# Attention with its probabilities turned on VectorE, values as 32x32 products in the scores' banks, and w_q and w_o streamed

## The chip, the cores and the metric

The kernel runs on one core of one Trainium2 chip. The metric is the device time of one launch in microseconds. Three runs of the kernel before took 1241.42 us in the median (1240.85 to 1242.42).

The engines are TensorE (in the profile PE for products and PEld for the loading of weights into the array), VectorE (DVE), ScalarE (ACT), GpSimd (POOL) and SyncE (SP), which issues all of this kernel's DMAs in one queue. Each engine works through its own instructions in the order in which the program gives them, and waits for others by semaphores. SBUF is the working memory with 128 partitions; PSUM, into which TensorE writes, has eight banks of 512 f32 columns in each partition.

## The reference, cut

All is f32. x is 4 sequences of 512 tokens with 1024 features; 32 query heads and 8 key/value heads of 32 features; 8 experts with low-rank weights of rank 16, of which each token uses 2.

```python
x = x + layernorm(attn(layernorm(x)))
x = x + layernorm(ffn(layernorm(x)))

def attn(x):
    q, k, v = split(x @ w_qkv.T + b_qkv)          # 1024, 256, 256 columns
    q, k = rope(q), rope(k)
    k, v = repeat(k, 4), repeat(v, 4)             # four query heads share one key head
    s = q @ k.T / sqrt(32), causal mask
    return (softmax(s) @ v) @ w_o.T + b_o

def ffn(x):
    top-2 gate over x @ gate_w.T; w = its softmax
    return x @ base_w.T + base_b + 2 * sum_e w[e] * (x @ A[e].T) @ B[e].T
```

## The kernel before

**Tiles.** A token tile is 128 tokens, 16 in all, four to a sequence. For each, TensorE computes keys and values (acc_kv), queries (acc_q, two halves of 512 columns), attention, the output projection (acc_o, two halves), the gate and low-rank inputs (acc_gl) and the base product (acc_f, two halves). Such a half is eight products of 128x128 weights-in-array by 512 columns, summed in one PSUM bank (`project`, L520 to L545). Activations are turned by TensorE against an identity before a projection (pt_xn, pt_h, pt_q, pt_k).

**Attention.** Heads are laid out so that a k tile (kt, two of them) holds four key heads, one on each quarter of the partitions, and a q tile holds one query head for each of these. `scores` (L1050) computes for a group of q tiles (four, two or one, as many as fill 512 columns with (i+1)*128 keys, where i is the token tile's place in its sequence): products of 32 rows, four side by side, into the tile sc of pool ps_sc. That is one tile of four banks, so one group of scores is alive at a time. VectorE masks the diagonal (L1119) and takes the negative maximum (L1129); ScalarE takes the exponentials into pr with their sum (L1079); VectorE inverts the sum (L1088); GpSimd multiplies (L1093). `turn` (L1138) turns pr on TensorE in 128x128 pieces (L1143) into a bank, and ScalarE or VectorE copies it to SBUF as prT (`copy`, L323 to L329). `values` (L1156) multiplies prT with v, 128 rows by 32 columns of the array, four heads side by side (L1166), and the result is copied to aT.

**Weights.** w_qkv and w_o are loaded whole once (`all_loads`, L1190). w_base is streamed: `Stream` (L393) loads pieces of 128x512 f32 (256 KB) into a ring of RING = 8, each as soon as a place is free; 256 pieces in all.

**Order.** The order of every engine is written out while the program is built. `Order` (L89) keeps a clock with an estimate for each instruction. TensorE's steps (`Step`, L79) stand in lanes: scores, turns of activations, values (with the turns of the probabilities), and dense products. `_choice` (L198) takes the first lane that is ready and `tensor` (L232) issues it; a score step and a ready value step go out as a pair (PAIRED). Instructions of the other engines are taken by urgency, then by age (`_next`, L138). Buffers are counted by `Slots` (L50): a chain takes a slot before it issues and gives it back when its last reader is done. BANKS = 4 PSUM banks outside the scores' serve all other products; SOFT = 10 tiles serve pr and prT.

Of the kernel before, what the change touches and what calls it, by code (L numbers as in the profile page):

```python
# [11 lines left out]
F32 = mybir.dt.float32  # L12
# [4 lines left out]
P = 128  # L17
# [15 lines left out]
PAIRED = 0.55  # L33
# [45 lines left out]
class Step:  # L79


    def __init__(self, us, issue, needs=(), bank=False, soon=()):
        self.us, self.issue, self.needs = us, issue, list(needs) + list(soon)
        self.tiled = False
        self.bank, self.soon = bank, soon
        self.done = Task()


class Order:  # L89
    ENGINES = ("dve", "act", "pool", "sp")  # L90

    def __init__(self, banks):
        self.now = self.at = 0.0
        self.free = dict.fromkeys(self.ENGINES, 0.0)
        self.waiting = {e: [] for e in self.ENGINES}
        self.seq = 0
        self.banks = banks
# [75 lines left out]
    def _ready(self, step):  # L173
        at = 0.0
        for t in step.needs:
            if t.at is None:
                return None
            at = max(at, t.at)
        if step.bank:
            if not self.banks.free:  # L180
                return None
            at = max(at, self.banks.free[0])
        return at

    def _take(self, step):
        if step.bank:
            heapq.heappop(self.banks.free)
        step.issue()

    def _is_ready(self, step):  # L190
        at = self._ready(step)
        return at is not None and at <= self.now

    def _comes(self, step):

        return all(t.at is not None for t in step.needs if t not in step.soon)

    def _choice(self, scores, values, lanes):  # L198

        later, ready, last = [], [], []  # L200
        score = scores[0] if scores else None


        value = values[0] if values and values[0].tiled else None
        waiting = []
        if score is not None and value is not None:
            if self._comes(score):
                waiting.append(values)
            if self._comes(value) and not self._is_ready(value):
                waiting.append(scores)  # L210
        for lane in lanes:
            at = self._ready(lane[0])
            if at is None:
                continue
            later.append(at)
            if at <= self.now:
                if any(lane is w for w in waiting):
                    last.append(lane)
                elif at + SAFE <= self.now:
                    return lane, None  # L220
                else:
                    ready.append(lane)
        if ready or last:
            return (ready + last)[0], None
# [7 lines left out]
    def tensor(self, scores, urgent, values, dense):  # L232


        while True:
            self.run(self.now)
            dense = [lane for lane in dense if lane]
            lanes = [lane for lane in [scores, *urgent, values] if lane]
            lanes += sorted(dense, key=lambda lane: lane[0].bank)
            if not lanes:  # L240
                break
            lane, at = self._choice(scores, values, lanes)
# [3 lines left out]
            steps = [lane.pop(0)]  # L246
            us = steps[0].us + TILING * steps[0].tiled
            if lane is scores and values and values[0].tiled and self._is_ready(values[0]):
                steps.append(values.pop(0))
                us = steps[0].us + steps[1].us + PAIRED  # L250
            for step in steps:
                self._take(step)
            self.now += us
            for step in steps:
                step.done.finish(self.now + FILL)
# [4 lines left out]
def kernel(  # L260
# [27 lines left out]
    BANKS, SOFT, RING = 4, 10, 8  # L288
# [7 lines left out]
    soft = ctx.enter_context(tc.tile_pool(name="soft", bufs=SOFT))  # L296
    weights = ctx.enter_context(tc.tile_pool(name="weights", bufs=RING))
# [6 lines left out]
    banks = Slots(BANKS)  # L304
    soft_slots, act_slots = Slots(SOFT), Slots(4)
    qT_slots, kT_slots, raw_slots, turn_slots = Slots(3), Slots(3), Slots(2), Slots(1)
    xa_slots, y_slots, w_slots = Slots(1), Slots(2), Slots(2)
    order = Order(banks)
# [42 lines left out]
    wqkv_sb = const.tile([P, ND, QKV], F32, name="wqkv_sb")  # L351
    rope_sb = const.tile([P, NQ, 2, HD], F32, name="rope_sb")
    bqkv_sb = const.tile([P, QKV], F32, name="bqkv_sb")
    wo_sb = const.tile([P, ND, D], F32, name="wo_sb")
# [13 lines left out]
    def chunks(name, w_sb, w, at, n):  # L368
        return [
            load(  # L370
                (name, at, c),
                P * n * 4 / 1024,
                w_sb[:, c, at : at + n],
                w[c * P : (c + 1) * P, at : at + n],
            )
            for c in range(ND)
        ]

# [10 lines left out]

    def part(w_sb, at, n):  # L390
        return lambda c: w_sb[:, c, at : at + n]

    class Stream:  # L393
# [10 lines left out]
        def __init__(self, w, n):  # L404
            self.w, self.n, self.slots, self.pieces = w, n, Slots(n), []

        def ask(self, c, cols):
            piece = self.Piece(self, self.w[c * P : (c + 1) * P, cols])
            self.pieces.append(piece)
            return piece  # L410

        def run(self, after):
# [4 lines left out]
            yield after  # L417
            for k, piece in enumerate(self.pieces):
                yield self.slots.take()

                def issue():
                    piece.sb = weights.tile([P, 512], F32, tag="piece", name=f"piece_{k}")
                    nc.sync.dma_start(out=piece.sb, in_=piece.in_)
# [4 lines left out]
    base_stream = Stream(w_base, RING)  # L428


    class Norm:
# [16 lines left out]
        def scale(self):  # L448
# [13 lines left out]

            yield dve(0.2, self.urgent, aggr)
            yield dve(0.15, self.urgent, eps)
            yield pool(0.6, 0, root)

        def apply(self, dst, src, h):
            cols = slice(h * 512, (h + 1) * 512)
            yield dve(
                0.7,  # L470
                self.urgent,
                lambda: nc.vector.tensor_scalar(  # L472
                    dst()[:, cols],
                    src()[:, cols],
                    self.mv[:, 0:1],
                    self.rstd,
                    ALU.subtract,
                    ALU.mult,
                ),
            )  # L480
# [13 lines left out]
    def transposes(dst, src, halves, name, slot):  # L494
# [3 lines left out]
        for h in range(NH):  # L498
# [17 lines left out]
            steps.append(Step(0.44, issue, [halves[h], slot], bank=True))  # L516
# [3 lines left out]
    def project(lhsT, w, n, name, needs, take, more=None):  # L520
# [20 lines left out]
        for c in range(ND + (more is not None)):  # L541
            us = 0.858 if n == 512 else 0.24
            steps.append(Step(us, partial(issue, c), needs[c], bank=(c == 0)))
# [3 lines left out]
    def rotated(acc, b_at, n, i, name, urgent, hold):  # L547
# [3 lines left out]
        yield raw_slots.take()  # L551
# [50 lines left out]
    class Tokens:  # L602
        def __init__(self, t):
# [3 lines left out]
            self.aT, self.has_aT = None, [Task() for _ in range(ND)]  # L607
# [46 lines left out]
    def load_y(tok):  # L654

        yield y_slots.take()
        yield has_wqkv
# [9 lines left out]
    def qkv(job, has_k, has_q):  # L667
# [6 lines left out]
        def normed():  # L674
# [4 lines left out]
            for h in range(NH):  # L679
                yield from norm.apply(lambda: job.xn, lambda: job.xn, h)  # L680
# [26 lines left out]
        def take_kv(acc, done):  # L707
# [3 lines left out]
            has_v = seq.has_v[i]  # L711

            def v_issue():
                seq.v[i] = kvpool.tile([P, KVD], F32, tag="v", bufs=6, name=f"v_{t}")
                nc.vector.tensor_add(
                    seq.v[i], acc[:, KVD : 2 * KVD], bqkv_sb[:, D + KVD : D + 2 * KVD]
# [3 lines left out]
            has_v.finish(order.at)  # L720
            yield from rotated(acc, D, KVD, i, f"k_{t}", 2, raw_k)
            k_ready.finish(order.at)

# [20 lines left out]
        step_k = Step(0.23, turn_k, [k_ready] + seq.kT_taken, bank=True)  # L744
        raw_q, q_ready = [[] for _ in range(NH)], [Task() for _ in range(NH)]

        def take_q(h, acc, done):
# [4 lines left out]
            yield qT_slots.take()  # L752
# [19 lines left out]
        steps_q = [Step(0.44, partial(turn_q, h), [q_ready[h]], bank=True) for h in range(NH)]  # L772

        def needs(at, n):
            return [
                [ready[c // 4]] + ([loaded["qkv", at, c]] if not t else []) for c in range(ND)
            ]

# [5 lines left out]
        products, turned = [], []  # L784
        if has_k:
            products += project(
                xnT, part(wqkv_sb, D, 2 * KVD), 2 * KVD, f"kv_{t}", needs(D, 2 * KVD), take_kv
            )
            turned.append(step_k)
        if has_q:  # L790
            for h in range(NH):
                products += project(
                    xnT,
                    part(wqkv_sb, h * 512, 512),
                    512,
                    f"q_{t}_{h}",
                    needs(h * 512, 512),
                    partial(take_q, h),
# [5 lines left out]
    def attention_out(tok):  # L804
# [50 lines left out]
        first = [loaded["o", 0, c] for c in range(ND)]  # L855
        steps = []
        for h in range(NH):
            needs = [
                ([tok.has_aT[ND - 2], slot] if not c else [tok.has_aT[c]])
                + ([first[c]] if not t else [])  # L860
                for c in range(ND)
            ]
            steps += project(
                lambda: tok.aT,
                part(wo_sb, h * 512, 512),
                512,
                f"o_{t}_{h}",
                needs,
                partial(take, h),
# [45 lines left out]
    def ffn(tok):  # L915
# [52 lines left out]
        step_low = Step(0.11, turn_low, [low_in], bank=True)  # L968
# [14 lines left out]
        def out_half(h):  # L983
            yield from norm.apply(lambda: tok.w, lambda: tok.w, h)
# [12 lines left out]
        def rest():  # L997
# [14 lines left out]
            part(wgl_sb, 0, GL),  # L1012
            GL,
            f"gl_{t}",
            [[r, loaded["gl"]] if not t else [r] for r in (ready[c // 4] for c in range(ND))],
            take_gl,
        )
        f = []
        for n in range(NH):
            cols = slice(n * 512, (n + 1) * 512)  # L1020
            chunks_n = [base_stream.ask(c, cols) for c in range(ND)]
            wants = [[ready[c // 4], chunks_n[c].here] for c in range(ND)]
# [332 lines left out]
```

## Time and profile before

| | us |
|---|---|
| median of three runs | 1241.42 |
| the profiled execution | 1241.56 |
| its span, first to last instruction | 1239.8 |
| PE busy | 1210.3 |
| DVE busy | 809.4 |
| POOL busy | 455.5 |
| ACT busy | 434.6 |
| HBM read | 97.94 MB |
| mean granted TensorE clock | 0.995 |

The span is what the profile covers. Busy times of an engine are the union of its instructions. The chain of waits is followed back from the last instruction to what released each one, so its shares tell which engine's work set the end. In a group's row, "128*32 128x128" means 128 rows by 32 columns of the array, 128 partitions by 128 columns streamed; "x2560" counts records, and an f32 product has two of them, one for each pass; the turns have one.

### The profile page before, as it was taken

The numbers are of one execution on the slowest core, as the hardware profiler recorded it, in microseconds if no ns is written. First come the engines' busy times: TensorE is split into PE (matmuls) and PEld (weight loads), VectorE is DVE, ScalarE is ACT, GpSimd is POOL, SyncE is SP. The second block draws the span as 40 slices with busy tenths as digits, with TensorE's granted clock in tenths as the row PEclk, the third lists the DMA queues.
The fourth block names the chain that finished last, engine by engine and source line by source line (L and its number), as shares of the span: only waits on it lengthen the run. The fifth ranks groups of instructions, "written<-read, shape, count | busy, mean of one in ns | idle before, by whom it ended". The sixth has DMA issues, their size and how long they took to land.

```text
span 1239.8 us, 20306 instructions
## 1 busy us (share of the span) xinstructions
PE 1210.3 (98%) x7416; PEld 658.6 (53%) x7416; DVE 809.4 (65%) x1673; ACT 434.6 (35%) x1360; POOL 455.5 (37%) x696
## 2 busy tenths in 40 slices
PE   7999999889999999999999999999999999999997
PEld 3555555445555555555555555555555555555543
DVE  3676766567657575866747667766666666777653
ACT  0343433334334333334444334323325333344400
POOL 1344434234154442424345334333234342434411
PEclk9999999999999999999999999999999999999999
DMA  9600050221410414113141140040411304105334
GB/s 359 248 18 17 2 165 23 69 77 43 136 52 8 145 36 133 55 36 119 35 128 61 52 137 17 15 148 26 136 52 52 120 1 136 35 23 163 131 110 152
DMA packets 54369, 107.63 MB, mean 87 GB/s; under 512 B 6400, under 2 KB 7424, under 8 KB 54272
## 3 DMA queue, kind: packets, MB, share of 16 engines
q1 hardware_dynamic: 54272, 106.36, 26.3%
q8 instruction: 59, 0.97, 0.3%
q14 instruction: 38, 0.31, 0.1%
HBM read 97.94 MB, written 8.39 MB: 86 GB/s over the span
## 4 chain that ended last, share of the span: by engine, by line
PE 95%; DVE 2%; ACT 1%; POOL 1%; issue 0%; DMA 0%; POOLq 0%; SPq 0%; ACTq 0%; DVEq 0%
PE acc_f L531 20%; PE acc_q L531 17%; PE acc_o L531 17%; PE pt_p L1143 12%; PE acc_kv L531 9%; PE sc L1058 7%; PE av L1166 6%; PE acc_gl L531 2%; PE pt_xn L505 1%; PE pt_h L505 1%; PE pt_q L758 1%; ACT pr L1079 1%; DVE nmax L1129 0%; PE pt_k L727 0%; DVE prT L328 0%
## 5 line engine op out<-in xcount | busy, mean ns | idle before, releaser
L1093 POOL TENSOR_SCALAR pr<-pr,rtot 128x256 f32<-128x256 f32 (+3 forms) x512 | 288.6, 577 | 519.5 <-DVE rtot L1088 426.6
L1079 ACT ACTIVATE pr<-sc,nmax 128x256 f32<-128x256 f32 (+3 forms) x512 | 263.5, 535 | 161.7 <-DVE nmax L1129 140.2
L531 PE MATMUL acc_f<-piece,T_h 128*128 128x512 f32 x512 | 236.5, 597 | 2.3 <-ACT prT L327 1.4
L531 PE MATMUL acc_o<-wo_sb,aT 128*128 128x512 f32 x512 | 233.3, 593 | 0.0
L531 PE MATMUL acc_q<-wqkv_sb,T_xn 128*128 128x512 f32 x480 | 220.7, 595 | 0.0
L1129 DVE TENSOR_REDUCE nmax<-sc 128x4 f32<-128x1536 f32 (+5 forms) x98 | 185.9, 1897 | 10.1 <-ACT pr L1079 8.4
L327 ACT COPY prT<-pt_p 128x512 f32<-128x512 f32 (+1 forms) x192 | 103.4, 551 | 245.8 <-PE pt_p L1143 240.1
L1143 PE MATMUL pt_p<-ident,pr 128*128 128x128 f32 x1280 | 177.0, 276 | 9.2 <-ACT prT L327 2.9
L1143 PEld LDWEIGHTS pt_p<-ident,pr 128*128 128x128 f32 x1280 | 146.6, 141 | 74.2 <-issue 63.3
L328 DVE COPY prT<-pt_p 128x512 f32<-128x512 f32 (+1 forms) x160 | 101.8, 637 | 62.4 <-PE pt_p L1143 59.6
L531 PEld LDWEIGHTS acc_o<-wo_sb,aT 128*128 128x128 f32 x512 | 92.4, 190 | 92.6 <-issue 91.3
L531 PEld LDWEIGHTS acc_f<-piece,T_h 128*128 128x128 f32 x512 | 91.7, 191 | 90.8 <-issue 84.8
L531 PEld LDWEIGHTS acc_q<-wqkv_sb,T_xn 128*128 128x128 f32 x480 | 86.3, 191 | 82.6 <-issue 80.9
L531 PE MATMUL acc_kv<-wqkv_sb,T_xn 128*128 128x512 f32 x256 | 119.1, 599 | 0.0
L1079 ACT ACTIVATION_READ_ACCUMULATOR pr<-sc,nmax 128x1 f32 x512 | 108.9, 213 | 0.0
L1058 PE MATMUL sc<-kT,qT 32*128 32x384 f32 (+3 forms) x1024 | 94.8, 468 | 0.0
L1088 DVE RECIPROCAL rtot<-total 128x1 f32<-128x1 f32 (+2 forms) x352 | 53.3, 158 | 61.4 <-ACT pr L1079 59.1
L487 POOL TENSOR_TENSOR y<-y,w 128x512 f32<-128x512 f32 x60 | 78.5, 1321 | 35.4 <-DVE w L472 35.4
L1166 PEld LDWEIGHTS av<-prT,v 128*32 128x32 f32 x2560 | 64.6, 109 | 50.0 <-issue 43.3
L1166 PE MATMUL av<-prT,v 128*32 128x128 f32 x2560 | 88.2, 276 | 0.0
L1119 DVE TENSOR_TENSOR sc<-sc,cmask 128x512 f32<-128x512 f32 (+3 forms) x98 | 83.7, 854 | 4.9 <-PE sc L1058 4.0
L461 POOL TENSOR_TENSOR rstd<-veps,neg_half 128x1 f32<-128x1 f32 x64 | 36.3, 567 | 125.1 <-DVE veps L457 111.3
(83 smaller groups left out, 898.9 us busy)
## 6 DMA issues: line engine op xcount, KB each, us to landing
piece<-in_w_base_dram SPq DMA_DIRECT2D x256, 256.0 KB, 3.4
xa<-in_x_dram SPq DMA_DIRECT2D x32, 256.0 KB, 3.0
y<-in_x_dram SPq DMA_DIRECT2D x16, 512.0 KB, 3.6
out_dram<-y SPq DMA_DIRECT2D x32, 256.0 KB, 2.0
wqkv_sb<-in_w_qkv_dram SPq DMA_DIRECT2D x8, 512.0 KB, 8.9
wo_sb<-in_w_o_dram SPq DMA_DIRECT2D x8, 512.0 KB, 7.3
wqkv_sb<-in_w_qkv_dram SPq DMA_DIRECT2D x8, 256.0 KB, 5.1
bqkv_sb<-in_b_qkv_dram SPq DMA_DIRECT2D x1, 768.0 KB, 7.7
```

The source lines that it names most:

```text
L327: act=(0.15 + n * 0.00085, lambda: nc.scalar.copy(out(), in_())),
L328: dve=(0.15 + n * 0.00105, lambda: nc.vector.tensor_copy(out(), in_())),
L487: engine.tensor_tensor(out=y()[:, cols], in0=y()[:, cols], in1=z()[:, cols], op=ALU.add)
L531: nc.tensor.matmul(acc[0][:, :n], lhsT=lhsT()[:, c, :] if c < ND else more[0](), rhs=w(c) if c < ND else more[1], start=(c == 0), stop=last,)
L1058: nc.tensor.matmul(sc[:, r, c * n : (c + 1) * n], lhsT=tok.qT[g.kt][rows, (g.at + c) % GROUP, :], rhs=seq.kT[g.kt][rows, :n], start=True, ...
L1079: lambda: nc.scalar.activation(pr[:, c * n : (c + 1) * n], sc4[:, r, c, :], AF.Exp, bias=nmax[:, r, c : c + 1], accum_out=total[:, r, c : ...
L1088: yield dve(0.17, 1, lambda: nc.vector.reciprocal(rtot[:, r, : g.n], total[:, r, : g.n]))
L1093: lambda: nc.gpsimd.tensor_scalar(pr[:, c * n : (c + 1) * n], pr[:, c * n : (c + 1) * n], rtot[:, r, c : c + 1], 1.0, ALU.mult, ALU.mult,),
L1119: lambda: nc.vector.tensor_tensor(out=diag, in0=diag, in1=cmask.unsqueeze(1).unsqueeze(1).to_broadcast([P, q, g.n, P]), op=ALU.add,),
L1129: lambda: nc.vector.tensor_reduce(nmax[:, some, : g.n], sc4[:, some], AX.X, ALU.max, negate=True),
L1143: nc.tensor.transpose(pt[:, j, :], g.pr[r][:, j * P : (j + 1) * P], ident)
L1166: nc.tensor.matmul(av[r * HD : (r + 1) * HD, c, :], lhsT=g.seq.v[j][:, head * HD : (head + 1) * HD], rhs=g.prT[r][:, c * (i + 1) + j, :], ...
```

## The change

- **Probabilities.** `turn` and its copies go. After the multiplication on GpSimd, VectorE's transpose instruction turns each 32x32 block of pr into z, the blocks staying where they are (`quadrant`). Four tiles z (one for each of the four heads of a k tile) hold all four q tiles of a k tile: pool zpool, one set of four.
- **Values.** One step for each k tile of a token tile (`Set`) in place of one for each group. For each block of 32 keys (4(i+1) of them) there are 16 products of 32x32 of the array by 128 columns: a quarter of the array's rows for each block of 32 queries, a quarter of its columns for each head. They write into a tile of ps_sc, so the scores' banks hold either a group of scores or a set of values. v has to lie on every quarter of the partitions: `spread` copies it with 16 DMAs of 32x256 for each token tile.
- **Weights.** w_q and w_o are streamed as w_base is, each through a ring of its own, RING = 6 for all three; only the key and value columns stay resident.
- **Norm.** It adds a negated mean where it subtracted the mean, and the pass over xa, and over w behind the ffn (but for the last tile), may run on GpSimd as well as on VectorE.
- **Order.** Score and value steps are no longer paired or held back for each other; values come first, then scores, then the rest. A projection starts only when there are slots for its results (`room_for`). Two inverses of the sums are taken at once (`totals`). The last two groups are no longer exchanged. SOFT goes from 10 to 8.

```diff
-    BANKS, SOFT, RING = 4, 10, 8
+    BANKS, SOFT, RING = 4, 8, 6
+    zpool = ctx.enter_context(tc.tile_pool(name="zpool", bufs=QUADS))
...
+    sc_slots, z_slots = Slots(1), Slots(QUADS)
...
-    wqkv_sb = const.tile([P, ND, QKV], F32, name="wqkv_sb")
+    wkv_sb = const.tile([P, ND, 2 * KVD], F32, name="wkv_sb")
-    wo_sb = const.tile([P, ND, D], F32, name="wo_sb")
...
+    streams = {"q": Stream("q", w_qkv), "o": Stream("o", w_o), "f": Stream("f", w_base)}
+
+    def streamed(name, at, steps):
+        pieces = streams[name].ask(at)
+        made = steps(lambda c: pieces[c].sb, [piece.here for piece in pieces])
+        for piece, step in zip(pieces, made):
+            start(piece.used(step.done))
+        return made
...
+            def minus():
+                self.nmean = small.tile([P, 1], F32, tag="nmean", bufs=4, name=f"nmean_{name}")
+                nc.vector.tensor_scalar_mul(self.nmean, self.mv[:, 0:1], -1.0)
...
+            on = {"dve": (0.7, partial(issue, nc.vector))}
+            if either:
+                on["pool"] = (0.8, partial(issue, nc.gpsimd))
+            yield Op(self.urgent, **on)
...
+        def spread(v):
+            seq.v[i] = kvpool.tile([P, QUADS, KVD], F32, tag="vq", bufs=6, name=f"vq_{t}")
+            for b in range(QUADS):
+                for r in range(QUADS):
+                    yield sp(
+                        0.09,
+                        lambda: nc.sync.dma_start(
+                            out=seq.v[i][r * HD : (r + 1) * HD, b, :],
+                            in_=v[b * HD : (b + 1) * HD, :],
+                        ),
+                    )
+            yield LANDS
+            seq.has_v[i].finish(order.at)
...
-            g.normed[r].finish(order.at)
+            yield g.set.has_room
+            at = (g.at % GROUP) * n
+            yield dve(
+                0.1 + g.n * n * 0.00105,
+                1,
+                lambda: nc.vector.transpose(g.set.z[r][:, at : at + g.n * n], pr[:, : g.n * n]),
+            )
+            soft_slots.give(order.at)
...
-    def turn(g, r):
...
-        for j in range(m):
-            nc.tensor.transpose(pt[:, j, :], g.pr[r][:, j * P : (j + 1) * P], ident)
...
-    def values(g):
+    def values(s):
...
-        av = ps.tile([P, GROUP, P], F32, tag="ps", name=f"av_{g.name}")
...
+        av = ps_sc.tile([P, QUADS, 512], F32, tag="sc", name=f"av_{s.name}")
+        nb = QUADS * (i + 1)
+        for b in range(nb):
+            for r in range(QUADS):
+                head = s.kt * GROUP + r
+                z = s.z[r][:, : GROUP * (i + 1) * P]
+                z = z.rearrange("p (c b q) -> p c b q", c=GROUP, b=nb)
+                for quad in range(QUADS):
+                    rows = slice(quad * HD, (quad + 1) * HD)
                     nc.tensor.matmul(
+                        av[r * HD : (r + 1) * HD, quad, :P],
+                        lhsT=s.seq.v[b // QUADS][rows, b % QUADS, head * HD : (head + 1) * HD],
+                        rhs=z[rows, :, b, :],
+                        start=(b == 0),
+                        stop=(b == nb - 1),
                     )
...
+            needs = [tok.has_q[one.kt]] + keys
+            older = k - 1 if m else k - 2
+            if older >= 0:
+                needs.append(sets[older].valued.done)
+            us = 0.218 * g.n * (tok.i + 1) + TILING
+            g.scored = Step(us, partial(scores, g), needs, bank=sc_slots)
+            score_lane.append(g.scored)
+        needs = [one.full, tok.aT_taken] + [tok.seq.has_v[i] for i in range(tok.i + 1)]
+        us = 0.92 * (tok.i + 1) + TILING
+        one.valued = Step(us, partial(values, one), needs, bank=sc_slots)
...
-    order.tensor(score_lane, turn_lanes, value_lane, dense_lanes)
+    order.tensor([value_lane, score_lane, *turn_lanes], dense_lanes)
```

## The prediction

> **What bounds the kernel now.** I read the page's busy shares and its chain of waits first, then the groups by shape, then one stretch of the timeline, the DMA issues, and a table of two tiny windows.
>
> ```profile
> PE 1210.3 (98%) x7416; PEld 658.6 (53%) x7416; DVE 809.4 (65%) x1673; ACT 434.6 (35%) x1360; POOL 455.5 (37%) x696
> PE 95%; DVE 2%; ACT 1%; POOL 1%; issue 0%; DMA 0%; POOLq 0%; SPq 0%; ACTq 0%; DVEq 0%
> PE acc_f L531 20%; PE acc_q L531 17%; PE acc_o L531 17%; PE pt_p L1143 12%; PE acc_kv L531 9%; PE sc L1058 7%; PE av L1166 6%; PE acc_gl L531 2%; PE pt_xn L505 1%; PE pt_h L505 1%; PE pt_q L758 1%; ACT pr L1079 1%; DVE nmax L1129 0%; PE pt_k L727 0%; DVE prT L328 0%
> ```
>
> TensorE (PE) is the chain: 95% of 1239.8 us. The turning of the probabilities (pt_p) is 12% of it, about 148 us, and all of that leaves TensorE with this change. The question is what comes next.
>
> ```profile
> 289.00 1.14 PE L1058 MATMUL sc<-kT,qT 32*128 32x512 f32 x8
> ...
> 290.20 0.70 DVE L1119 TENSOR_TENSOR sc<-sc,cmask 128x512 f32<-128x512 f32 x1
> 290.94 2.29 DVE L1129 TENSOR_REDUCE nmax<-sc 128x4 f32<-128x2048 f32 x1
> ...
> 293.56 1.07 ACT L327 COPY prT<-pt_p 128x512 f32<-128x512 f32 x2 [0.71 <-PE pt_p L1143]
> ...
> 294.52 0.70 ACT L1079 ACTIVATE pr<-sc,nmax 128x512 f32<-128x512 f32 x1
> ...
> 295.73 0.59 ACT L327 COPY prT<-pt_p 128x512 f32<-128x512 f32 x1 [0.41 <-PE pt_p L1143]
> ...
> 298.12 0.22 ACT L1079 ACTIVATION_READ_ACCUMULATOR pr<-sc,nmax 128x1 f32 x1
> ...
> 299.86 1.14 PE L1058 MATMUL sc<-kT,qT 32*128 32x512 f32 x8
> ```
>
> This is one group of scores (one of four q tiles of a k tile, 512 keys) in the timeline of all engines. It holds the scores' four banks from 289.00 to 298.34, 9.34 us, and the next group can't start before. The reader is to see the parts: product, wait for VectorE, mask, maximum, wait for ScalarE (busy with prT copies), four exponentials with another prT copy between. Taking all 88 groups from the timeline the same way, the mean hold is 16.3 us (128 keys, 8 groups), 12.7 (256, 16), 8.9 (384, 32) and 10.2 (512, 32): 945 us of banks in use. Before, that has slack against TensorE.
>
> ```profile
> L1143 PE MATMUL pt_p<-ident,pr 128*128 128x128 f32 x1280 | 177.0, 276 | 9.2 <-ACT prT L327 2.9 <-DVE rtot L1088 2.7 <-POOL pr L1093 2.6
> L1166 PE MATMUL av<-prT,v 128*32 128x128 f32 x2560 | 88.2, 276 | 0.0
> L328 DVE COPY prT<-pt_p 128x512 f32<-128x512 f32 x96 | 66.2, 690 | 41.0 <-PE pt_p L1143 40.4
> L328 DVE COPY prT<-pt_p 128x384 f32<-128x384 f32 x64 | 35.6, 558 | 21.5 <-PE pt_p L1143 19.2
> ```
>
> Those are the groups by shape (busy us, mean ns of one, then idle time before it). Next, windows of the value products alone (length; PE; PEld), and the row of the streamed weights among the DMA issues (median us to landing):
>
> ```profile
> 76.36:76.38 0.03, 0.02 (x4) 0.02 (x4) 0.00 (x0) 0.00 (x0) 1.00 0.00 0
> 76.39:76.48 0.09, 0.09 (x4) 0.09 (x8) 0.00 (x0) 0.00 (x0) 1.00 0.00 0
> ```
> ```profile
> piece<-in_w_base_dram SPq DMA_DIRECT2D x256, 256.0 KB, 3.4
> ```
>
> Four value products are on within the first 0.03 us, and no more of them in the next 0.09. So four tiles of 32 columns do run side by side, each start some 7 ns after the last, and then the array is full until a pass has streamed.
>
> **TensorE's part of the change.** 1280 transposes go. The dense products stay: 928 of 0.858 us (eight in 6.87 us in the chain's list) and 128 short ones of 0.24, 827 us; the other 432 transposes at 0.109 are 47. Scores: 320 blocks (128 queries by 128 keys by 4 heads) at 0.218, 70 us. Values before: 320 at 0.218. After: 320 times 16 products of half as many rows; 16 starts 7 ns apart are 0.11 us, just the time a pass of 128 columns streams, and f32 takes two passes (records are twice the instructions), so 0.23 a block, 74 us. Nothing before shows 16 tiles at once, only 4 by rows (scores) and 4 by columns (values). Bounds: 0.22, all together, and 0.87, four at a time, which adds 205 us; I take 0.23, as both kinds of four are shown and the starts fit. Changes of shape: before, score and value steps go out in pairs, 0.33 us idle into the values and 0.20 out of them, so 0.55 a pair, 88 pairs; after, 88 + 32 steps of 0.4: 48 us each, no difference. Sum before 827+47+140+70+70+48 = 1202, and 1066 after.
>
> A rule of the Trainium skill speaks against this: "TensorE: Matmul & The Clock Gate", section "Wait — 56ns, not 53.3ns?", says that two matmuls never start closer together than some 25 ns. By it, 10,240 passes would take an estimated 256 us, 182 more than my term. The window above shows four starts within 0.03 us, so for tiles that don't share a part of the array the row decides.
>
> **The banks' part.** Values now take the scores' banks, 32 times. In the changed kernel's TensorE order I counted the work in each of the 120 stretches from one holder of the banks to the next (88 score groups, 32 value sets). Where that work is shorter than the hold, TensorE idles. A typical stretch of 512 keys has eight to ten dense products, 8 to 9.5 us; some have none (three near the end; others where two steps for the banks follow each other). Behind a late step for the banks stand the next dense products on TensorE, and behind those VectorE's adds of their biases. What is the hold? At its least, from the rows: 1.14 + 0.15 + 0.69 + 2.29 + 0.1 + 2.97 = 7.5 us for 512 keys, and 6.1, 9.1 and 14.0 for the others. At most as measured, 10.2, 8.9, 12.7, 16.3. To each I add 0.35 for handing over; a value set holds its products plus 1.85 (change of shape, signal, copy to aT of 0.69, handing over). Summing the larger of work and hold over the stretches: 1132 with the least holds, 1155 midway, 1214 with those of before. The same sum for the old order gives 1208 midway against a span of 1239.8, so 32 us (start-up loads, tail, missed waits) are outside it; those stay.
>
> Which hold? ScalarE loses 192 prT copies (103 us), which alone delayed the group above by about 1.9 us. Of z there is one set of four tiles, so a transpose waits for the values of the set before, and behind it on VectorE stands the next mask: late values make late masks. VectorE gets 352 transposes of 32x32 blocks, 128 of 384 and 224 of 512 columns; no row shows one. Nearest are VectorE's copies of the same size, 0.558 and 0.690: 226 us. Below, 0.62, the norm's 512-column pass; above, twice the copy, +226 us, if blocks pass at half rate. I take the copy. Off it: prT copies 102, aT 6, half of the reciprocals 25, 28 norm passes that go to GpSimd 18; on it: 65 negated means at 0.15, 10, and 2 for other copies. VectorE: 809 + 226 - 139 = 896 us, 74%. In a stretch of 512 keys that is 0.69 + 2.29 + 4 x 0.69 + 0.32 and 2.8 of norms and adds, 8.9 us in 9.3: tight, so waits before the mask (1.9 us now) don't vanish. One effect shortens, one lengthens: midway.
>
> **Weights.** 512 more pieces of 256 KB, and 256 small copies of v, all on SP's queue. A ring of 6 gives 6 x 0.86 = 5.1 us against 3.4 us to land, 1.7 us spare (8 pieces: 3.5). Waits for pieces cost TensorE 2.9 us before; three times the pieces, 9. The issues take 0.33 us each in SP's rows, so 16 v copies block 5.2 us: where pieces stand behind all of them, 3.5 us late, 16 times, 56 us. Between 9 and 56 I take 15, as the order mixes them and pieces wait behind few. 224 MB over 1200 us is 187 GB/s against 359 in the first slice. GpSimd gets 28 passes of 0.74, 21 us, in a 37% share: hidden by its idle time; without that cover the norms come later and the dense lanes with them.
>
> **Sum.** 1066 + 89 (banks) + 32 + 15 = 1202 span; the median is 1.6 above the profiled span (1241.42, 1239.8): 1204 us.
>
> **Rivals.** (1) *The banks come free sooner*: without ScalarE's copies the holds reach their least. 1132 + 32 + 9 + 2 = 1175, down to 1155 if starting waits shrink too. For: the 1.9 us above. Against: VectorE's 74%. 17%. (2) *The banks become the bound* (the other side): VectorE's transposes stand before the next mask, holds stay as before or grow, and values are added on top. 1214 + 32 + 15 + 2 = 1263. It decides from holds at about 87% of the way from least to measured, 9.8 us at 512 keys. For: 945 us in use already. 20%. (3) *Weights late behind v copies*: 1204 + 41 = 1245. 7%. (4) *16 products don't all overlap*: eight at a time +70, four +205: 1275 to 1410. Against: the 7 ns. 8%.
>
> **Numbers.** Forecast 48% (1180 to 1235). A measurement tells 0.2%, 2.5 us, from none. Faster: 47 of the forecast's, 16 of rival 1's, 63%. Same 5% (edges of forecast, 2 and 3). Slower 32%. Range 1155 to 1265: beyond it lie most of rival 4 (7%), the worst of 2 (6%), and 3% below.
>
> **What would show it.** Right: no pt_p; value rows 0.23 us a block; TensorE's busy time near 1075 us, and idle of 80 to 120 before sc or av, ended by ACT pr or the aT copy; holds at 512 keys near 8.8. Transposes of 0.6 to 0.7. Waits for w_q, w_o, w_f pieces under 20 us. Wrong: value steps of 2 us a token tile and more; transposes over 1 us with VectorE above 90%; mask waits over 2.5 us.

## The result, and the profile after

The changed kernel took 1414.28 us in the median of four runs (1409.3 to 1418.65) against 1241.13 for the kernel before: a ratio of 1.139, with an interval of 1.135 to 1.144. The forecast was 1204 (1155 to 1265). It is slower by 173 us and lies 210 above the forecast, outside the range.

Four parts of the page of the changed kernel answer to those of before: busy time, granted clock in 40 slices, and the chain by engine and by line.

```profile
PE 1210.0 (86%) x13816; PEld 610.5 (43%) x13816; DVE 872.7 (62%) x1691; ACT 329.6 (23%) x1147; POOL 473.0 (33%) x724
PEclk9999899889999999799999999998989999976899
PE 70%; DMA 8%; issue 8%; DVE 7%; SPq 3%; ACT 3%; POOL 2%; POOLq 0%; ACTq 0%; DVEq 0%
PE acc_f L506 15%; PE acc_o L506 13%; PE av L1204 12%; PE acc_q L506 12%; PE acc_kv L506 7%; PE sc L1085 5%; DMA w_q<-in_w_qkv_dram 4%; DVE nmax L1177 3%; DMA w_o<-in_w_o_dram 2%; ACT pr L1105 2%; SPq L706 2%; PE acc_gl L506 2%; DVE z L1133 1%; PE pt_h L480 1%; PE pt_q L747 1%
```

pt_p is gone and with it 177 us of TensorE's busy time, yet TensorE is as busy as before (1210 us) and has 197 us of gaps between its products besides. The chain's new shares name the places: av 12% (it was 6%), DMA 8%, "issue" 8% (an engine that waits for nothing the profile shows), SP's queue 3%.

The groups by shape of the values and of VectorE's transposes (busy us, mean ns of one, then idle time before it and who ended it):

```profile
L1204 PE MATMUL av<-z,vq 32*32 32x128 f32 x10240 | 173.8, 315 | 104.9 <-issue 78.1 <-ACT pr L1105 22.9 <-DVE stats L411 3.7
L1133 DVE STREAM_TRANSPOSE z<-pr 128x512 f32<-128x512 f32 x224 | 149.0, 693 | 38.8 <-PE av L1204 23.4 <-POOL pr L1119 14.6
L1133 DVE STREAM_TRANSPOSE z<-pr 128x384 f32<-128x384 f32 x128 | 69.4, 563 | 16.1 <-PE av L1204 9.5 <-POOL pr L1119 5.9
```

The transposes cost what was forecast (0.69 and 0.56 us). The values don't. One set of 12 key blocks in TensorE's timeline (start, length, records, idle before):

```profile
855.47 3.14 PE L1204 MATMUL av<-z,vq 32*32 32x128 f32 x222
861.36 1.90 PE L1204 MATMUL av<-z,vq 32*32 32x128 f32 x128 [2.76 <-issue]
865.11 0.69 PE L1204 MATMUL av<-z,vq 32*32 32x128 f32 x34 [1.84 <-issue]
```

Two things are to be seen. A stretch of 128 records, four blocks, takes 1.90 us where 0.92 was forecast. And the set stops twice, for 2.76 and 1.84 us; the second stop comes 128 records after the first, which are 256 instructions, as each product has a loading of its weights. Over all 32 sets, from first to last record of each, the values take 252 us: 1.9 for a set of 4 blocks, 4.8 to 7.3 of 8, 8.7 to 11.3 of 12, 12.6 to 14.9 of 16. The group above splits this in two: 174 us busy, and 78 us of gaps ended by "issue", which are such stops. (The other 27 us of its idle time lie before sets.) The forecast was 74 us. The waits of PE have the stops as one row (us in total, times, longest), and the page's list of DMA queues has the transfers that bring instructions (number, MB, share of the DMA engines):

```profile
PE av L1204 <- issue: 78.1, 46, 3.2
q8 instruction: 108, 1.77, 0.5%
```

The second row settles what the stops are. 1.77 MB in 108 transfers are 16 KB each; 108 times 256 instructions are 27,648, and TensorE's products and loadings are 27,632, so this queue feeds TensorE. In the packed trace, counting TensorE's products and loadings from the start of the program, all 46 stops lie at the same place in a batch of 256 (after the 193rd or 194th), and each ends 1.2 to 1.6 us after one of these transfers has landed. So a stop is a wait for the next 256 instructions; what fills the time from the landing to the next product is not shown.

The other loss stands in the waits of the weight loads (us in total, times, longest):

```profile
PEld av L1204 <- issue: 110.4, 71, 3.4
PEld acc_q L506 <- DMA w_q<-in_w_qkv_dram: 40.0, 43, 4.1
PEld acc_o L506 <- DMA w_o<-in_w_o_dram: 32.4, 33, 5.1
PEld acc_f L506 <- DMA w_f<-in_w_base_dram: 5.3, 9, 1.9
```

Waits for pieces are 78 us, mostly for w_q and w_o. SP's own timeline shows why at one place:

```profile
51.75 1.14 SPq L706 DMA_DIRECT2D vq<-v  x2
52.98 0.53 SPq L380 DMA_DIRECT2D w_q<-in_w_qkv_dram  x1
53.55 1.14 SPq L706 DMA_DIRECT2D vq<-v  x2
54.79 0.53 SPq L380 DMA_DIRECT2D w_q<-in_w_qkv_dram  x1
55.36 0.51 SPq L706 DMA_DIRECT2D vq<-v  x1
55.97 0.53 SPq L380 DMA_DIRECT2D w_q<-in_w_qkv_dram  x1
```

Two copies of v and one piece are 1.8 us of SP, one copy and one piece 1.2, and TensorE uses a piece in 0.86. While copies are mixed with pieces like this, SP's issuing is slower than TensorE's using.

### The profile page after: what moved, and what is told of

Same layout as the page of the kernel before. It is cut to its first block, busy times and chain, and to the rows that moved or that the text cites. A ratio compares the mean times of both kernels' runs of the same rounds, so it can differ in the third digit from the quotient of the medians.

```text
span 1415.0 us, 33584 instructions
## 1 busy us (share of the span) xinstructions
PE 1210.0 (86%) x13816; PEld 610.5 (43%) x13816; DVE 872.7 (62%) x1691; ACT 329.6 (23%) x1147; POOL 473.0 (33%) x724
## 2 busy tenths in 40 slices
DMA packets 138136, 242.75 MB, mean 172 GB/s; under 512 B 18432, under 2 KB 27648, under 8 KB 137984
## 3 DMA queue, kind: packets, MB, share of 16 engines
q8 instruction: 108, 1.77, 0.5%
## 4 chain that ended last, share of the span: by engine, by line
PE 70%; DMA 8%; issue 8%; DVE 7%; SPq 3%; ACT 3%; POOL 2%; POOLq 0%; ACTq 0%; DVEq 0%
PE acc_f L506 15%; PE acc_o L506 13%; PE av L1204 12%; PE acc_q L506 12%; PE acc_kv L506 7%; PE sc L1085 5%; DMA w_q<-in_w_qkv_dram 4%; DVE nmax L1177 3%; DMA w_o<-in_w_o_dram 2%; ACT pr L1105 2%; SPq L706 2%; PE acc_gl L506 2%; DVE z L1133 1%; PE pt_h L480 1%; PE pt_q L747 1%
## 5 line engine op out<-in xcount | busy, mean ns | idle before, releaser
L1204 PE MATMUL av<-z,vq 32*32 32x128 f32 x10240 | 173.8, 315 | 104.9 <-issue 78.1
L506 PE MATMUL acc_o<-w_o,aT 128*128 128x512 f32 x512 | 242.5, 619 | 17.9 <-DMA w_o<-in_w_o_dram 16.5
L1133 DVE STREAM_TRANSPOSE z<-pr 128x512 f32<-128x512 f32 (+1 forms) x352 | 218.4, 646 | 54.8 <-PE av L1204 32.8
L506 PE MATMUL acc_f<-w_f,T_h 128*128 128x512 f32 x512 | 243.9, 616 | 3.1 <-DMA w_f<-in_w_base_dram 3.0
L506 PE MATMUL acc_q<-w_q,T_xn 128*128 128x512 f32 x480 | 226.1, 608 | 17.7 <-DMA w_q<-in_w_qkv_dram 17.6
L1204 PEld LDWEIGHTS av<-z,vq 32*32 32x32 f32 x10240 | 138.1, 111 | 152.8 <-issue 110.4
L506 PEld LDWEIGHTS acc_o<-w_o,aT 128*128 128x128 f32 x512 | 96.8, 197 | 144.4 <-issue 106.0
L506 PEld LDWEIGHTS acc_f<-w_f,T_h 128*128 128x128 f32 x512 | 95.1, 195 | 115.0 <-issue 105.7
L506 PEld LDWEIGHTS acc_q<-w_q,T_xn 128*128 128x128 f32 x480 | 87.2, 193 | 129.9 <-issue 85.6
L506 PE MATMUL acc_kv<-wkv_sb,T_xn 128*128 128x512 f32 x256 | 120.8, 612 | 0.0
```

The lines of the kernel that those rows point to most:

```text
L506: nc.tensor.matmul(acc[0][:, :n], lhsT=lhsT()[:, c, :] if c < ND else more[0](), rhs=w(c) if c < ND else more[1], start=(c == 0), stop=last,)
L1133: lambda: nc.vector.transpose(g.set.z[r][:, at : at + g.n * n], pr[:, : g.n * n]),
L1204: nc.tensor.matmul(av[r * HD : (r + 1) * HD, quad, :P], lhsT=s.seq.v[b // QUADS][rows, b % QUADS, head * HD : (head + 1) * HD], rhs=z[rows ...
```

## The experiments

Two theories stood against each other for the values. S: the cost is in the number of instructions. A: it is in the array, by shapes and columns streamed. For the weights, V: v's copies hold the pieces up; its rivals were the rings' length (R) and the DMA rate (B). W is the theory that streaming and late weights are what costs. All runs had the kernel before beside them, at 1241.7 to 1243.4 us. The two kernels in bf16 were timed four times each; every other run below is a single one, and the four times of the changed kernel lie within 10 us.

**Fewer columns.** All blocks of values but the first stream 32 of their 128 columns.

```diff
+                    m = GROUP if b == 0 else 1
...
-                        av[r * HD : (r + 1) * HD, quad, :P],
+                        av[r * HD : (r + 1) * HD, quad, : m * HD],
...
-                        rhs=z[rows, :, b, :],
+                        rhs=z[rows, :m, b, :],
```

> The changed kernel with every value product still issued, but only the first block of 32 keys streams its 128 columns; the later blocks stream 32 (the first q tile of the four). It leaves out the later blocks' share of three q tiles of four in the values. Theory S (instruction supply: a value step takes the time in which its 64 instructions a block reach TensorE, 0.43 us a block, and a wait at each 16 KB of instructions): nothing changes, value steps together 257 us, total 1400 to 1425 us. Theory A (the array: the 16 tiles do not stream together): the columns streamed fall from 320 x 128 to 32 x 128 + 288 x 32, a third, so value steps together about 85 us and the total 1240 to 1290 us. Theory W (weights that come late are what costs): 1400 to 1425 us, as S.

1420.67 us: no gain from a quarter of the streaming. Sets took 236 us in place of 252, with stops of 115 in place of 78; those of 4 blocks, which have no stop, 1.44 to 1.60 in place of 1.90. Busy time fell by 53 us and the stops grew by 37. So columns set part of the pace inside a stretch, but most of what they save is spent waiting at the next stop: for the stops, theory S.

**Fewer blocks.** Every second block of keys, then all but the first, left out of the values.

```diff
-        for b in range(nb):
+        for b in range(0, nb, 2):
```

> The changed kernel with every second block of 32 keys left out of the values: half of the value products and half of their instructions, the order of everything else the same. S: a step of 128 keys 0.9 us in place of 1.9; a step of 512 keys has two pages of instructions in place of four, 5 to 7 us in place of 13 to 15; value steps together 105 to 125 us and the total 1230 to 1290 us. A: exactly half, 128 us, total 1270 to 1300 us. W: waits for pieces of w_q and w_o stay near 70 us and the total stays above 1350 us.

```diff
-        for b in range(nb):
+        for b in range(1):
```

> The changed kernel with one block of 32 keys alone in the values, 16 products in place of 64 to 256, the order of everything else the same: all that the change does except the value products. S: value steps together about 15 us; the banks are free sooner too; total 1130 to 1190 us, below the kernel before. A: the same. W, and the rival that VectorE's transposes or the banks hold the rest back: waits for w_q and w_o, or holds of the banks above 9 us at 512 keys, keep it above 1240 us.

1264.13 and 1227.13 us. Half of the blocks took 150 us with it (sets 101 us in place of 252, stops 17 in place of 78); the other half, but for one block, only 37. More of a set of half the length fits into what has been fetched before it. In the second step the sets shrank by 84 us (101 to 17) where the time fell by 37: other waits took the rest up, those for w_q and w_o pieces growing from 81 to 96 us. The second run, above its expectation, showed a cause apart from the values: with sets of 17 us in all the kernel still lay 97 us over the sum of the forecast without values (1130).

**Sets cut in parts**, each of four blocks, with dense products between where some are ready.

```diff
+PART, PAUSE = 4, 1.0
...
-        for b in range(nb):
+        for b in range(part * PART, (part + 1) * PART):
```

> The changed kernel with a value step cut into parts of four blocks (256 instructions, 16 KB), the next part not before 1 us after the last has ended, so that dense products can stand between; in about half of the places there are two or three of them. Nothing is left out. S: parts with dense products before them take 1.8 us without a break, the breaks of 1 to 2 us inside value steps fall from about 100 us to 40 to 60 us, total 1330 to 1385 us. A: the parts take no less each than their share before (3.5 us for four blocks) and the changes of shape add some 15 us, total 1410 to 1440 us. W: as A.

1413.02 us: a miss by the time, though the stops inside values fell from 78 to 22 us, as S has it. The time went into other waits: values for the exponentials 48 us (before 23), weight loads for w_q and w_o pieces 90 (before 72), with the order of everything else changed by the edit. A part of four blocks with nothing to run beside it is as slow as ever, and the banks are held as long. So the stops can be hidden, but not by this alone.

**The same number of products in the kernel before.** Its value products, 128 rows by 32 columns, each cut into four of 32 streamed columns: 16 a block as in the changed kernel, all columns streamed.

```diff
+            for q0 in range(0, P, HD):
...
-                        rhs=g.prT[r][:, c * (i + 1) + j, :],
+                            rhs=g.prT[r][:, c * (i + 1) + j, q0 : q0 + HD],
```

> The kernel before, with each of its value products (128 rows by 32 columns, 128 columns streamed) cut into 4 products of 32 streamed columns: 16 products a block in place of 4, as in the changed kernel, the same columns streamed, nothing left out. Theory S (TensorE takes an instruction in about 6.8 ns, so 16 products of f32, 64 instructions, cost 0.433 us a block): a block costs 0.35 to 0.45 us in place of 0.22 once the instructions fetched ahead are used up, 1270 to 1310 us. Rival A (what is slow in the changed kernel is that its tiles have only 32 rows and sit side by side in both directions): a block stays near 0.24 us, 1241 to 1252 us.

1269.39 us, 26 more than before. A group of 4 blocks (one of 56 has a stop) takes 1.30 us where it took 1.08: 0.32 a block, between the two theories. Its starts settle at 8.3 to 9.1 ns from one record to the next in the mean, not at the 13.5 (two instructions of 6.8) that I had put down to instructions. The run with fewer columns shows 8.3 between stops, and so does the bf16 run below. So in these TensorE keeps up some 4.2 ns an instruction, and the 13.5 ns of the changed kernel between stops (0.433 us for a block of 32 records) is not the supply of instructions: it goes with f32 passes of 128 columns on 16 tiles. They take 0.217 us for each of the two passes of a block, twice the 0.109 of a pass before. Why they do is open.

**Streaming alone**, in the kernel before: w_q and w_o through rings of 6.

```diff
-    BANKS, SOFT, RING = 4, 10, 8
+    BANKS, SOFT, RING = 4, 10, 6
...
+    q_stream = Stream(w_qkv, RING, "q")
+    o_stream = Stream(w_o, RING, "o")
```

> The kernel before with one part of the change alone: w_q and w_o streamed through rings of 6 pieces, as w_base, all in SP's one queue; only key and value columns resident. Probabilities, values and norms as before. Theory W (streaming by itself is dear: three rings behind one another in one queue bring pieces late, and TensorE's clock falls with the waits): waits of TensorE for w_q, w_o and w_f pieces of 30 to 70 us in all, time 1270 to 1310 us. Rival W0 (streaming is cheap as predicted; the late pieces of the changed kernel come from the copies of v and the output stores that stand before them): under 15 us of waits, 1240 to 1256 us.

1254.08 us, 11 more, with these waits:

```profile
PEld acc_o L542 <- DMA w_o<-in_w_o_dram: 8.0, 13, 2.0
PEld acc_q L542 <- DMA w_q<-in_w_qkv_dram: 7.6, 9, 2.8
PEld acc_f L542 <- DMA w_f<-in_w_base_dram: 2.9, 5, 1.1
```

W0 by the time; the waits, 18.5 us, lie a little over its 15 and far under W's 30 to 70. 224 MB read from memory over 1252 us cost little by themselves. The forecast of 15 us fits this kernel.

**No streaming beside cheap values.** The run with one block, w_q and w_o resident, 4 of v's 16 copies.

> The run with one block of 32 keys in the values (1227 us), with w_q and w_o resident again; of the copies of v only the 4 for the first block are made, and the turned probabilities of all groups go to the same 512 columns; the output is incomplete, as it was there. Theory W (of the 97 us by which that run lay above my sum less its values, 1130, the larger part is streaming): no waits for w_q and w_o, a clock of 0.97 or more, 1140 to 1175 us. Rival (the scores' banks, the norms and changes of shape are what is left): 1190 to 1225 us.

1146.1 us, 81 less than with streaming and copies, as W expected; the granted clock, 0.95, stayed under its 0.97. This is near the forecast's sum without its weights' term and with these short sets: 1204 - 74 - 15 + 17 = 1132. So banks, norms and order together cost what was forecast, within 14 us.

**v's copies by ScalarE's queue**, in the changed kernel.

```diff
-                    yield sp(
+                    yield act(
...
-                        lambda: nc.sync.dma_start(
+                        0,
+                        lambda: nc.scalar.dma_start(
```

> The changed kernel, with the 16 copies of v of each token tile issued by ScalarE's queue rather than SP's; nothing left out. Theory V (the copies, which wait for VectorE's sum of v and then take 16 issues, hold up the pieces behind them on SP): TensorE's waits for w_q and w_o pieces fall from 72 us to under 35, time from 1414 to 1365 to 1395 us. Rival (the pieces are late for other reasons: the rings are short, or the output stores stand before them): waits of 60 us and more, time 1400 to 1425 us.

1457.1 us: a miss, and of no use as a test. A copy takes ScalarE 0.60 us, in front of exponentials: values waited 61 us for ACT pr, before 32. Pieces were late as before (71 us), and now SP stood 92.5 us waiting for vq copies to land, which it had not done. Why the pieces' issues wait for them there is open.

**v's copies last in SP's queue.** They are priced at 0.59 us and given out only where no piece waits; first in the run with one block, then in the whole changed kernel.

```diff
-                    yield sp(
-                        0.09,
+                    yield Op(
+                        5,
+                        sp=(0.59, lambda b=b, r=r: nc.sync.dma_start(
```

> The same edit of the order of v's copies in the run with one block of 32 keys in the values (1227 us; output incomplete as there). Theory V: most of the 81 us between that run and the one with resident weights comes back: 1150 to 1185 us, waits for w_q and w_o under 25 us. Rival: 1205 us and more.

> The changed kernel with the copies of v priced in SP's order at the 0.59 us that one took and given out only where no piece waits, still in SP's queue (the six tiles vq and the two tiles v are counted as slots, so that the order can't block itself). Nothing left out. Theory V (the copies stand between pieces: one piece and two copies take 1.8 us of SP where TensorE uses a piece in 0.86): waits for w_q and w_o pieces fall from 72 us to under 25, time from 1414 to 1340 to 1380 us. Rival (rings of 6 are too short, or DMA is too slow at 170 to 190 GB/s): waits stay above 55 us, time 1400 us and more.

1189.61 us (from 1227.13) and 1383.13 (from 1414.28), each 3 to 5 us above V's range and some 16 under the rival's. In the changed kernel the waits fell from 72 to 30 us:

```profile
PEld acc_o L507 <- DMA w_o<-in_w_o_dram: 17.5, 34, 2.9
PEld acc_q L507 <- DMA w_q<-in_w_qkv_dram: 12.1, 15, 2.2
```

V holds in kind, below its size (the waits too stayed above its 25 us: 30, and 59 beside cheap values): the order of the copies gives back 38 of the 81 us beside cheap values and 31 in the whole kernel.

**Rings of 10** in the run with one block and v's copies last.

```diff
-    BANKS, SOFT, RING = 4, 8, 6
+    BANKS, SOFT, RING = 4, 8, 10
```

> The run with one block of values and v's copies last (1190 us), with rings of 10 pieces in place of 6; the turned probabilities of all groups go to the same 512 columns, as in the run with resident weights (1146 us); output incomplete as there. Theory R (of the 44 us left between these two, the most is that 6 pieces ahead are too few where stores and loads stand between pieces): waits for w_q and w_o fall from 59 us to under 20, 1150 to 1172 us. Rival B (the DMA engines are the limit, at 195 GB/s): waits above 40 us, 1180 to 1195 us.

1167.13 us:

```profile
PEld acc_q L507 <- DMA w_q<-in_w_qkv_dram: 7.3, 9, 1.7
PEld acc_o L507 <- DMA w_o<-in_w_o_dram: 3.5, 9, 0.8
```

Theory R: 59 us of waits for w_q and w_o (96 before v's copies went last) became 11, at the same bytes. Of the 81 us, 38 are the place of v's copies, 22 the rings' length. The last 21 are not named; part stands in a wait of k's turn for VectorE (25 us, one of 19.7), an order that this run has and the resident one has not.

**Half of the instructions, nothing left out.** Probabilities and v in bf16, v's copies last: a product is one pass, 5,120 in place of 10,240, on the same tiles with the same columns. It is less exact than f32.

```diff
-            pr = soft.tile([P, GROUP * P], F32, tag="soft", name=f"pr_{g.name}_{r}")
+            pr = soft.tile([P, GROUP * P], BF16, tag="soft", name=f"pr_{g.name}_{r}")
```

> The run with v's copies last, with probabilities (pr, z) and v held in bf16, so that a value product is one pass: 5120 products become 5120 pairs of instructions in place of 10,240, and the same tiles, the same 128 columns; nothing left out, but less exact than f32. Theory S (a step of values is slow by its instructions: a block takes 0.22 us at best and, past the two pages fetched ahead, waits for a fetch at every 256 instructions): a set of 16 blocks, 512 instructions, takes 3.5 to 6 us, the sets 70 to 110 us in all in place of 257; with the pieces on time 1180 to 1240 us. Rival A (the cost is in the 16 tiles' columns and shapes alone, and halves with the passes): sets 125 to 135 us in all, 1240 to 1290 us.

1229.96 us (1227.74 to 1233.38), a ratio of 0.990 to the kernel before, interval 0.988 to 0.992. Sets took 93 us in all (29 of them stops, 7 waits for v's copies), as S expected, where A expected 125 to 135. This is one of 16 blocks in the timeline:

```profile
275.71 2.75 PE L1209 MATMUL av<-z,vq 32*32 32x128 bf16 x218 [2.30 <-ACT pr L1110]
280.15 0.63 PE L1209 MATMUL av<-z,vq 32*32 32x128 bf16 x38 [1.69 <-issue]
```

The first stretch has twice as many blocks as the f32 one above. That it has nearly the same number of records (218, there 222) is chance: in the changed kernel first stretches run from 154 to 363 records, by where the set begins in a batch of 256 instructions. What is the same is the place of the stops in the program: here too all 11 lie after the 193rd or 194th of 256, and end 1.3 to 1.5 us after a transfer of 16 KB landed; so do the 49 of the run with fewer columns and the 11 of the run with half of the blocks. A stop therefore goes by instructions and not by columns or blocks, which is S.

> The run with bf16 probabilities and v, v's copies last (1230 us), with rings of 10 in place of 6, for which bf16 leaves room; nothing else changed. Theory R: the 43 us of waits for w_q and w_o fall to under 15, 1190 to 1215 us. Rival B: 1222 us and more.

With rings of 10, 1221.79 us (1220.02 to 1226.12), ratio 0.983, interval 0.982 to 0.985. Waits for w_q and w_o fell from 43 to 13 us, as R has it; the time, 8 us lower, lies 0.2 us under B's range and 7 above R's; values waited more for vq copies (13.2 us, before 8.3). It is the fastest kernel here that leaves nothing out, 20 us under the one before, at the price of bf16.

## Why the prediction was wrong, step by step

*Values: the step that failed.* "16 starts 7 ns apart are 0.11 us, just the time a pass of 128 columns streams, ... so 0.23 a block, 74 us." The 7 ns were read from one four of records; in the kernel before they hold inside each four, and the next four starts 0.11 us after the first. In the changed kernel they hold for the first 32 records of a set only. In a window of 0.25 us at the start of the set shown above there are 32 records, one block; the next blocks take 0.43:

```profile
855.46:855.71 0.25, 0.24 (x32) 0.24 (x33) 0.00 (x0) 0.00 (x0) 1.00 1.08 360
```

The spacing of a burst was read as a rate. A steady block costs 0.43 us at full clock, and the sets were busy for 174 us with what the half clock added. On top came what the sum had no term for: 78 us of stops at every 256 instructions. Four blocks of keys, which are 256 instructions, take 1.9 us, while in sets with several stops the next 256 landed 3.3 to 4.7 us after the last: behind its first stretch a long set goes by this feed. By the runs, the blocks after the first of each set cost 187 us (1414 against 1227), where the forecast had 74 - 17 = 57: 130 us of the miss. (The sets alone shrank by 235 us; part of that came back as other waits.) Rival 4, that 16 products don't all overlap (8%, 1275 to 1410), had the place right; its bound of 205 us was for another mechanism, and the result lies 4 us beyond it. The rule of starts 25 ns apart, which I set aside, gave 256 us for the values and they took 252. But that is not how it came about: starts lay 6.7 ns apart in the burst and 13.5 after it, and 78 us were stops.

*Weights: mis-sized.* 15 us were forecast, 81 measured beside cheap values: 66 us of the miss. Each copy of v held SP 0.59 us and not the 0.33 of other rows, 153 us in all, and "the order mixes them and pieces wait behind few" was the error: just this mixing, one or two copies between each two pieces, made SP slower than TensorE. By the runs that is 38 of the 81 us; 22 are the rings, whose 1.7 us to spare was too little; 21 stay open. Rival 3 had the mechanism, at 41 us and 7%.

*Banks: right.* The holds, read as before, are 8.3, 7.0, 11.1 and 15.3 us (512, 384, 256 and 128 keys), where 8.8 was forecast for 512 keys and midway was 7.5, 10.9 and 15.1 for the others. In the run with 1146 us, where the sets and late pieces don't stretch the rest, they are 8.7, 7.0, 10.6 and 14.6. Waits before the mask, which the forecast expected to stay, fell to 0.3 to 1.0 us from 1.7 to 3.4 (in that run 0.5 to 0.8); which of the copies that VectorE and ScalarE lost did this was not tried. The parts of the least hold for 512 keys add up to 7.3 us and not to the 7.5 written there. That 1146 us were measured where this sum gives 1132 is the test of it.

*VectorE: right.* 0.563 and 0.693 us a transpose against 0.558 and 0.690; 873 us in all against 896.

*The clock: no term.* The granted clock fell from 0.995 to 0.93. Dense products took 28 us longer in all (919 us against 890, adding up the groups). This is not a further cause but a part of the price of the gaps above. In the run with 1146 us the same groups take 4 us more than before, so it is a small part of the last 14 us. The three misses, 130, 66 and 14, make up the 210, as they must: each is a difference of single runs against the forecast, and another order of leaving things out would share them out otherwise (v's copies gave 38 us beside cheap values and 31 in the whole kernel).

## What to carry to other kernels

A spacing of starts read from a few tiny instructions need not be one that can be kept up: look for a run of several hundred, and count instructions, 256 to a fetch. Before moving work into many small instructions, ask what hides the fetch: 64 f32 products in a row (256 instructions) cost no stop in the changed kernel, sets of 128 and more did. Small DMAs in the queue of a weight stream are priced by their issue (0.59 us here) times the pieces that stand behind them; give them out last, and make the ring longer than the longest thing that can stand between two pieces.

## What the runs showed of the hardware

**Fetching instructions can stop TensorE.** In each of eight runs every stop inside the values that "issue" ended (46 in the changed kernel, up to 3.2 us) lies at the same place in a batch of 256 TensorE instructions and ends 1.1 to 1.6 us after a transfer of 16 KB of instructions has landed. Inside one set such transfers landed 3.3 to 4.7 us apart. The Trainium skill, page "Runtime: NRT & Kernel Launch", section "Instruction fetch mechanics", says that instructions are refilled in blocks of 256, and that crossing such a block is mostly hidden since engines dispatch more slowly than the refill. The size of the block agrees with the trace; that it is hidden doesn't: 46 stops, 78 us.

**The clock can halve after a window that is far from idle.** The records of the clock change on a grid of 3.41 us. In four windows of the changed kernel that lie on it within 0.1 us (length, PE busy, PEld busy and so on; the last three numbers are clock, DMA share, GB/s):

```profile
859.50:862.91 3.41, 1.55 (x122) 1.44 (x128) 0.00 (x0) 0.00 (x0) 0.00 (x0) 1.00 0.24 87
862.91:866.32 3.41, 1.57 (x63) 0.78 (x47) 0.48 (x1) 0.00 (x0) 0.00 (x0) 0.99 0.00 0
866.32:869.73 3.41, 3.41 (x12) 1.13 (x10) 1.82 (x5) 0.00 (x0) 0.00 (x0) 0.51 0.37 106
869.73:873.14 3.41, 3.41 (x15) 1.44 (x8) 3.38 (x6) 0.00 (x0) 0.00 (x0) 1.00 0.51 179
```

In the second, PE was busy for 1.57 of 3.41 us, 46%, without one gap of that length, and the next window ran at half the clock. The first, at 45%, kept the full clock. Over the changed kernel's whole trace all 25 drops followed a window with PE busy for 48% or less, and each window under 43% was followed by one; seven between 43 and 48% were not, so this share alone does not decide there. In the run with fewer columns one window of 58% lost the clock. At half clock, windows of up to 84% still left it there. Before, 13 us of the span were at half clock, after, 197. The skill's page "TensorE: Matmul & The Clock Gate", section "Part 1: The HAM clock gate (the "warmup" mystery)", has the window of 3.4 us and the half rate, and gives an idle window as the condition; here windows of up to 48% busy were followed by half clock.
